# A relational graph convolution on one core: edge counts per group alone on TensorE, counts per relation from the slot table

## The chip, the cores and the metric

The kernel runs on one core of a Trainium2 chip. The core has five engines with a queue each, which run at the same time and wait for each other through semaphores: TensorE (PE in the profile; its weight loads are PEld), VectorE (DVE), ScalarE (ACT), GpSimd (POOL) and SyncE (SP, which here only starts transfers). Matrix products are written by TensorE into PSUM, which has eight banks, and are read from there by VectorE and ScalarE. The metric is the device time of one execution in microseconds; the time before is the median of three executions.

## The reference

For 1250 nodes with 1024 features and 20,000 edges of 8 relations, the kernel computes one graph layer with a gate and a residual. Cut to what matters:

```
h = relu(layernorm(x))
u = h @ root + bias
for r in range(8):
    mask = (edge_type == r)
    sums = segment_sum(h[src] * mask, dst)          # over the edges of relation r
    cnt  = segment_sum(mask, dst)                   # edges of relation r into each node
    u   += (sums / max(cnt, 1)) @ weight[r]
z = concat([u, h]) @ w_gate + b_gate
out = x + tanh(u) * z + h * (1 - z)
```

The edges are only known at run time, so the kernel sorts them itself: that is its index.

## The kernel before

**Products.** The kernel multiplies first and gathers then: for every relation it forms y = h @ weight[r] for all nodes (and h @ root, h @ w_gate), stores the rows of y in HBM, and each node then gathers the rows of its edges and adds them with the weight 1/cnt. There are eleven matrices of 1024 x 1024 (eight relations, root, two halves of the gate), numbered s. The ten blocks of 128 nodes go in five pairs, numbered i. One (s, i) is a `step`; its product is done with Strassen's seven half-size products, partly nested a second time (lines 210 to 360), in fp32. A step calls `between(j)` after each of its sub-products; there the generators that stand for all other work (the index, later the gathering) are moved on by one `yield`. What a generator issues between two yields thus lands in every engine's queue right behind that sub-product. The order of every queue is the program's own order; nothing reorders it.

**Two groups.** Relations 0 to 4 are group 0, relations 5 to 7 group 1 (`R0 = (0, 5, 8)`), so that gathering from group 0 can run while group 1 is multiplied. Each (group, node) is a key. Each key has a row of `SLOTS` = 28 places in a table in HBM; an edge's place is key x row width + the edge's rank among the edges of its key. The row of the table had 8 more words (`WIDE` = 36), into which the reciprocals of the relation counts were stored.

**The index.** `columns` prepares the edges as 157 columns of 128 edges: `key_col`, `row_col` (which row of y) and `tb_col` (relation x 10 + block of the target node). `slots` then goes over the columns in 40 rounds of `CG` = 4. For one group j of four columns it issues, over several rounds:

- `one_hots`: ScalarE makes `is_lo` (which of 128 low parts of the key), VectorE makes `is_at` (which of 20 high parts, line 1020, and which of 80 relation-blocks, line 1020 too).
- `count`: TensorE multiplies the one-hots, 4 matmuls of 100 columns (line 1031), into PSUM bank `ps_n`: the edges of each key and of each relation and node in each column. VectorE adds them to the running sum `seen` (line 1036), four additions, one after the other.
- `as_int`, `split`, `as_bf16`: the running sum before each column is cut into two bf16 parts, with casts on ScalarE (1051, 1053, 1066) and two masks on VectorE (1059).
- `place`: TensorE looks the sums up for each edge, 4 matmuls of 40 columns (line 1082), into PSUM bank `ps_q`. VectorE picks each edge's own value (1087, 1091), counts the equal keys ahead of it in its column (1096), and forms its place `at_i` (1099 to 1106). GpSimd scatters the four columns into the table (1110). `at_i` has two buffers.

In one round the order is: `as_bf16(j-3)`, `one_hots(j)`, the load of the keys, `as_int(j-2)`, a yield, `count(j-1)`, `split(j-2)`, `place(j-3)`, `to_los(j-2)`, a yield. So on TensorE four count matmuls and four look-up matmuls, of different groups of columns, stand one behind the other. The rounds run beside the steps of s = 0 to 3, from about 107 to 417 us.

**After it.** `order` ranks the nodes by their number of edges, stores the reciprocals of the relation counts into the table (line 1149, SP) and gathers each node's table row, in rank order, into `idx`. `weights(g)` turns `idx` into a weight for each slot on VectorE (`slot_weights`, lines 730 to 743). From s = 5 on, `edges` gathers rows of y (line 1294, GpSimd) and adds them (line 1299, VectorE) beside the products. `passes_needed` works out whether a node has more edges than slots; a runtime branch (line 1441: every engine loads the number, line 1443: and branches) skips the code for that case, which this data doesn't need. `got()` hands out one of five scratch tiles.

## Time and profile before

| | |
|---|---|
| median of 3 runs | 1348.01 us (1346.19 to 1349.48) |
| profiled execution, its own time | 1347.63 us |
| its span, first to last instruction | 1345.6 us |
| VectorE, ScalarE, GpSimd busy | 74%, 29%, 43% of the span |
| VectorE busy in the index rounds, 107 to 417 us | 236.0 of 310.0 us |
| ScalarE busy in the same stretch | 177.2 of 310.0 us |
| VectorE busy from 417 to 506 us, and from 506 to 625 us | 49.8 of 89.0 us, and 59.4 of 119.0 us |
| GpSimd's table scatters end; its next work starts | 419.8 us; 457.1 us |
| first gather of y rows | 635.1 us |
| granted TensorE clock, mean | 0.998 |

A line of a timeline has the start in us, the busy time in us, the engine, the source line, the operation, the tile written and the tiles read, sizes, the number of instructions merged, and in brackets how long the engine had been idle and what released it. A line of the groups has the same names, then busy time in us and the mean duration of one instruction in ns, and the idle time before them by releaser. A matmul's duration includes its way through the array: matmuls overlap, so what one costs TensorE is the distance to the start of the next.

### The profile page before, as it was taken

How to read it: one execution, taken by the hardware profiler on the slowest of the kernel's cores; microseconds unless marked ns; L12 is line 12 of the kernel's file. 1: busy time of each engine (PE TensorE's matmuls, PEld its weight loads, DVE VectorE, ACT ScalarE, POOL GpSimd, SP SyncE). 2: the span in 40 equal slices, each digit the busy share in tenths (PEclk: the TensorE clock that was granted, in tenths of full speed). 3: DMA queues.
4: the chain of work that ended last, by engine and by line, in shares of the span. 5: the costliest groups of instructions: out<-in, count | busy, mean ns of one | idle time of the engine just before them, and what ended most of it. 6: DMA issues, size and time to landing. Idle time of an engine off the chain costs nothing.

```text
span 1345.6 us, 13662 instructions
## 1 busy us (share of the span) xinstructions
PE 1332.0 (99%) x4098; PEld 712.2 (53%) x4098; DVE 995.7 (74%) x2049; ACT 384.0 (29%) x852; POOL 579.9 (43%) x511
## 2 busy tenths in 40 slices
PE   9999999999999999999999999999999999999997
PEld 5444455455445545655654565565556556554443
DVE  7855976876784937524887978887788799867875
ACT  3335656565641111111221211112122111221210
POOL 0001755655563346101444646336354655625631
PEclk9999999999999999999999999999999999999999
DMA  8744665844673162133739778867878967879961
GB/s 313 271 181 145 105 135 148 209 81 124 160 183 83 49 171 53 48 126 122 234 114 349 223 254 326 310 230 268 286 260 291 343 211 234 288 275 283 345 171 59
DMA packets 106910, 271.17 MB, mean 202 GB/s; under 512 B 22692, under 2 KB 24946, under 8 KB 106704
## 3 DMA queue, kind: packets, MB, share of 16 engines
q1 hardware_dynamic: 46640, 120.01, 29.2%
q0 software_dynamic: 44064, 118.28, 27.9%
q10 hardware_dynamic: 16128, 31.98, 7.2%
q8 instruction: 32, 0.52, 0.2%
q14 instruction: 46, 0.38, 0.1%
HBM read 212.71 MB, written 75.66 MB: 214 GB/s over the span
## 4 chain that ended last, share of the span: by engine, by line
PE 79%; issue 7%; DMA 7%; DVE 4%; POOL 3%; ACT 0%; POOLq 0%; DVEq 0%; ACTq 0%
PE ps_b L405 40%; PE ps L405 17%; PE ps L218 11%; DMA got<-y,idx 5%; PE ps_n L405 3%; PE ps_b L218 2%; PE ps_q L218 2%; PE ps_q L405 1%; DVE u L1299 1%; PE ps_n L218 1%; POOL got L1294 1%; DMA got<-hr_dram,node 1%; PE ps L370 1%; DMA hr_dram<-row 1%; POOL out_dram L720 1%
## 5 line engine op out<-in xcount | busy, mean ns | idle before, releaser
L405 PE MATMUL ps_b<-w,h_op 128*128 128x512 f32 x1560 | 701.9, 595 | 1.0 <-ACT row L484 0.8
L405 PEld LDWEIGHTS ps_b<-w,h_op 128*128 128x128 f32 x1560 | 291.6, 190 | 329.2 <-issue 318.7
L1294 POOL DMA_INDIRECT got<-y,idx x193 | 246.3, 1276 | 326.4 <-DVE u L1299 195.8
L1299 DVE SCALAR_TENSOR_TENSOR u<-got,w_of,u 128x1024 f32<-128x1024 f32 (+1 forms) x193 | 247.1, 1283 | 33.8 <-DMA got<-y,idx 31.1
L405 PE MATMUL ps<-w,h_op 128*128 128x512 f32 (+1 forms) x592 | 263.4, 588 | 1.0 <-ACT row L464 1.0
L1110 POOL DMA_INDIRECT table<-row_col,at_i x157 | 177.7, 1132 | 156.4 <-DVE at_i L1106 70.3
L405 PEld LDWEIGHTS ps<-w,h_op 128*128 128x128 f32 x592 | 111.3, 190 | 125.0 <-issue 120.8
L430 DVE TENSOR_TENSOR row<-row 128x512 f32<-128x512 f32 x53 | 36.7, 693 | 72.9 <-ACT row L429 72.7
L429 ACT COPY row<-ps_b 128x512 f32<-128x512 f32 x53 | 31.0, 585 | 197.4 <-PE ps_b L405 193.4
L514 ACT COPY row<-ps_b 128x512 f32<-128x512 f32 x49 | 28.6, 584 | 200.3 <-PE ps_b L405 171.5
L405 PE MATMUL ps_n<-w,h_op 128*128 128x512 f32 x176 | 80.1, 592 | 0.0
L218 PE MATMUL ps<-w,w 128*128 128x256 f32 x288 | 71.5, 381 | 0.3 <-DVE w L211 0.3
L484 ACT COPY row<-ps_b 128x512 f32<-128x512 f32 x54 | 31.6, 586 | 135.9 <-PE ps_b L405 131.1
L218 PE MATMUL ps<-w,h_op 128*128 128x256 f32 x264 | 68.3, 381 | 0.0
L218 PEld LDWEIGHTS ps<-w,w 128*128 128x128 f32 x288 | 54.2, 190 | 21.9 <-issue 14.6
L1036 DVE TENSOR_TENSOR seen<-seen,ps_n 128x100 f32<-128x100 f32 x157 | 40.3, 257 | 30.1 <-PE ps_n L1031 10.1
L218 PEld LDWEIGHTS ps<-w,h_op 128*128 128x128 f32 x264 | 49.6, 190 | 24.3 <-issue 18.7
L1096 DVE SCALAR_TENSOR_TENSOR junk<-k_bc,key_col,before 128x128 f32<-128x128 int32 x157 | 55.1, 351 | 4.2
L453 ACT COPY row<-ps_b 128x512 f32<-128x512 f32 x54 | 31.7, 587 | 90.9 <-PE ps_b L405 82.9
L405 PEld LDWEIGHTS ps_n<-w,h_op 128*128 128x128 f32 x176 | 33.4, 190 | 39.5 <-issue 38.7
L464 ACT COPY row<-ps 128x512 f32<-128x512 f32 x37 | 21.6, 585 | 105.2 <-PE ps L405 92.6
L173 DVE TENSOR_TENSOR w<-w,w 128x2048 f32<-128x2048 f32 (+1 forms) x12 | 25.4, 2115 | 35.1 <-PE ps L405 34.9
(244 smaller groups left out, 1530.6 us busy)
## 6 DMA issues: line engine op xcount, KB each, us to landing
y<-row SPq DMA_DIRECT2D x72, 512.0 KB
w<-in_L_gnn_weight_dram ACTq DMA_DIRECT2D x21, 1024.0 KB
w<-in_L_gnn_weight_dram SPq DMA_DIRECT2D x10, 1024.0 KB
k_bc<-keys_dram SPq DMA_DIRECT2D x39, 256.0 KB
l_bc<-los_dram SPq DMA_DIRECT2D x39, 256.0 KB
w<-in_L_gnn_w_gate_dram ACTq DMA_DIRECT2D x6, 1024.0 KB
h_dram<-h_op SPq DMA_DIRECT2D x9, 512.0 KB
u<-in_L_gnn_bias_dram SPq DMA_DIRECT2D x9, 512.0 KB
```

The costliest lines, as they stand in the source:

```text
L218: nc.tensor.matmul(p, a[:, k, :], b[:, k, :], start=(fresh and k == 0), stop=(k == 1), skip_group_check=True)
L405: nc.tensor.matmul(b[:, at], aop[:, i, k, :], w.of[i][:, k, at], start=(fresh and k == 0), stop=(k == KQ - 1), skip_group_check=True)
L429: nc.scalar.copy(d, b)
L430: nc.vector.tensor_add(c22, c22, d)
L453: nc.scalar.copy(c11, b)
L484: nc.scalar.copy(c12, b)
L514: nc.scalar.copy(c21, b)
L1036: nc.vector.tensor_add(seen[j][:, i, :], was, p[:, i, :])
L1096: nc.vector.scalar_tensor_tensor(junk, o["k_bc"][:, i, :], key_col[:, c:c + 1], before, op0=OP.is_equal, op1=OP.mult, accum_out=rank[:, c: ...
L1110: ins = nc.gpsimd.indirect_dma_start(out=table[:, :], out_offset=bass.IndirectOffsetOnAxis(ap=at_i[:n, i:i + 1], axis=0), in_=row_col[:n, ...
L1294: nc.gpsimd.indirect_dma_start(out=t[:n], out_offset=None, in_=y[g][:, :], in_offset=bass.IndirectOffsetOnAxis(ap=at[:n, d, k:k + 1], axis=0),
L1299: nc.vector.scalar_tensor_tensor(u[:n], t[:n], w, u[:n], op0=OP.mult, op1=OP.add)
```

## The change

The count matmul keeps the 20 columns of the keys only. The counts per relation are no longer made on TensorE; they come from the table rows in `idx`: since the table holds row numbers of y, which grow with the relation, the number of slots with a value of at least r x 1250 is counted on VectorE for each relation (`slot_counts`, one compare and one reduction each). Edges beyond the 28 slots are added by `counts_over`, behind a second runtime branch at the last step of s = 4. `tb_col`, the reciprocals in the table and their stores are gone; the table's row is 28 words. The running sum's two bf16 parts are now a rounded copy (ScalarE) and the rest (VectorE, `residue`). The last small operations of the rank are done for four rounds at once (`to_table`, `AT` = 4), and `at_i` is one tile for all columns. Counts and look-ups both write to parts of one PSUM bank, `q_bank` (the bank `ps_q`).

The rounds, as a diff:

```diff
+        q_bank = psum.tile([P, CG, P], F32, name="ps_q", bufs=1).rearrange("p c k -> p (c k)")
...
+            counted = q_bank[:, H:H + CG * NHI].rearrange("p (c b) -> p c b", b=NHI)
+            looked = q_bank[:, H + CG * NHI:H + 3 * CG * NHI].rearrange(
+                "p (c a b) -> p c a b", a=2, b=NHI)
...
@@ -1014,28 +1024,23 @@
                                          bias=less_lo[:, c0 + i:c0 + i + 1])
                 nc.scalar.activation(is_lo[:, :m, :], is_lo[:, :m, :], AF.Relu, scale=-1.0,
                                      bias=1.0)
-                is_at = ix.tile([P, CG, NHI + NTB], BF16, name="is_at", bufs=4)
-                for t, of, width in ((is_at[:, :, :NHI], hi_col, NHI),
-                                     (is_at[:, :, NHI:], tb_col, NTB)):
-                    nc.vector.tensor_tensor(t[:, :m, :],
-                                            of[:, c0:c1, None].to_broadcast([P, m, width]),
-                                            io[:, None, :width].to_broadcast([P, m, width]),
-                                            op=OP.is_equal)
+                is_at = ix.tile([P, CG, NHI], BF16, name="is_at", bufs=4)
+                nc.vector.tensor_tensor(is_at[:, :m, :],
+                                        hi_col[:, c0:c1, None].to_broadcast([P, m, NHI]),
+                                        io[:, None, :NHI].to_broadcast([P, m, NHI]),
+                                        op=OP.is_equal)
                 now[j] = dict(is_lo=is_lo, is_at=is_at)
 
             def count(j):
                 cs, o = chunks(j), now[j]
-                m = len(cs)
-                p = psum.tile([P, CG, P], F32, name="ps_n", bufs=1)[:, :, :NHI + NTB]
-                for i in range(m):
-                    nc.tensor.matmul(p[:, i, :], o["is_lo"][:, i, :], o["is_at"][:, i, :],
+                for i in range(len(cs)):
+                    nc.tensor.matmul(counted[:, i, :], o["is_lo"][:, i, :], o["is_at"][:, i, :],
                                      start=True, stop=True)
-                seen[j] = ix.tile([P, CG, NHI + NTB], F32, name="seen", bufs=3)
-                for i in range(m):
-                    was = seen[j][:, i - 1, :] if i else seen[j - 1][:, CG - 1, :]
-                    nc.vector.tensor_add(seen[j][:, i, :], was, p[:, i, :])
+                for i, c in enumerate(cs):
+                    nc.vector.tensor_add(seen[:, c % RING, :], seen[:, (c - 1) % RING, :],
+                                         counted[:, i, :])
                 if j == ng - 1:
-                    nc.vector.tensor_copy(runs, seen[j][:, m - 1, :])
+                    nc.vector.tensor_copy(runs, seen[:, cs[-1] % RING, :])
 
             def load_keys(j):
                 c0, m = j * CG, len(chunks(j))
@@ -1044,26 +1049,26 @@
                     nc.sync.dma_start(t[:, :m, :].rearrange("p c e -> p (c e)"),
                                       of[None, c0 * P:(c0 + m) * P].to_broadcast([P, m * P]))
 
-            def as_int(j):
+            def parts_seen(j):
 
                 m = len(chunks(j))
-                s_i = now[j]["s_i"] = ix.tile([P, CG, NHI], I32, name="s_i")
-                nc.scalar.copy(s_i[:, 0, :], seen[j - 1][:, CG - 1, :NHI])
-                if m > 1:
-                    nc.scalar.copy(s_i[:, 1:m, :], seen[j][:, :m - 1, :NHI])
-
-            def split(j):
-                m, o = len(chunks(j)), now[j]
-                s_2 = o["s_2"] = ix.tile([P, CG, 2, NHI], I32, name="s_2")
-                for a, mask in enumerate((-P, P - 1)):
-                    nc.vector.tensor_single_scalar(s_2[:, :m, a, :], o["s_i"][:, :m, :], mask,
-                                                   op=OP.bitwise_and)
+                k = (j * CG - 1) % RING
+                return [(0, k, 1), (1, 0, m - 1)] if k == RING - 1 else [(0, k, m)]
 
             def as_bf16(j):
 
-                m, o = len(chunks(j)), now[j]
-                s_b = o["s_b"] = ix.tile([P, CG, 2, NHI], BF16, name="s_b")
-                nc.scalar.copy(s_b[:, :m], o["s_2"][:, :m])
+                s_b = now[j]["s_b"] = ix.tile([P, CG, 2, NHI], BF16, name="s_b", bufs=3)
+                for to, k, n in parts_seen(j):
+                    if n:
+                        nc.scalar.copy(s_b[:, to:to + n, 0], seen[:, k:k + n])
+
+            def residue(j):
+
+                s_b = now[j]["s_b"]
+                for to, k, n in parts_seen(j):
+                    if n:
+                        nc.vector.tensor_sub(s_b[:, to:to + n, 1], seen[:, k:k + n],
+                                             s_b[:, to:to + n, 0])
 
             def to_los(j):
 
@@ -1076,48 +1081,49 @@
             def place(j):
                 cs, o = chunks(j), now.pop(j)
                 m, c0 = len(cs), cs[0]
-                c1 = c0 + m
-                p = psum.tile([P, CG, P], F32, name="ps_q", bufs=1).rearrange("p c k -> p (c k)")
                 for i in range(m):
-                    nc.tensor.matmul(p[:, i * 2 * NHI:(i + 1) * 2 * NHI], o["to_lo"][:, i, :],
+                    nc.tensor.matmul(looked[:, i].rearrange("p a b -> p (a b)"),
+                                     o["to_lo"][:, i, :],
                                      o["s_b"][:, i].rearrange("p a b -> p (a b)"),
                                      start=True, stop=True)
-                q = p[:, :CG * 2 * NHI].rearrange("p (c a b) -> p c a b", a=2, b=NHI)
                 own = ix.tile([P, CG, 2, NHI], F32, name="own", bufs=1)
                 nc.vector.tensor_tensor(
-                    own[:, :m], q[:, :m],
-                    o["is_at"][:, :m, None, :NHI].to_broadcast([P, m, 2, NHI]), op=OP.mult)
-                o2 = ix.tile([P, CG], F32, name="o2")
-                nc.vector.reduce_sum(o2[:, :m], own[:, :m].rearrange("p c a b -> p c (a b)"),
-                                     axis=AX.X)
+                    own[:, :m], looked[:, :m],
+                    o["is_at"][:, :m, None, :].to_broadcast([P, m, 2, NHI]), op=OP.mult)
+                nc.vector.reduce_sum(base[:, c0:c0 + m],
+                                     own[:, :m].rearrange("p c a b -> p c (a b)"), axis=AX.X)
 
                 for i, c in enumerate(cs):
                     junk = ix.tile([P, P], F32, name="junk", bufs=1)
                     nc.vector.scalar_tensor_tensor(junk, o["k_bc"][:, i, :], key_col[:, c:c + 1],
                                                    before, op0=OP.is_equal, op1=OP.mult,
                                                    accum_out=rank[:, c:c + 1])
-                nc.vector.tensor_add(rank[:, c0:c1], rank[:, c0:c1], o2[:, :m])
-                over = ix.tile([P, CG], F32, name="over")
-                nc.vector.tensor_single_scalar(over[:, :m], rank[:, c0:c1], float(SLOTS),
-                                               op=OP.is_ge)
-                at = ix.tile([P, CG], F32, name="at")
-                nc.vector.tensor_add(at[:, :m], first[:, c0:c1], rank[:, c0:c1])
-                at_i = ix.tile([P, CG], I32, name="at_i")
-                nc.vector.scalar_tensor_tensor(at_i[:, :m], over[:, :m], float(FAR), at[:, :m],
+                if j % AT == AT - 1 or j == ng - 1:
+                    to_table(j // AT * AT * CG, c0 + m)
+
+            def to_table(c0, c1):
+                at = slice(c0, c1)
+                m = c1 - c0
+                nc.vector.tensor_add(rank[:, at], rank[:, at], base[:, at])
+                over = ix.tile([P, AT * CG], F32, name="over", bufs=1)
+                nc.vector.tensor_single_scalar(over[:, :m], rank[:, at], float(SLOTS), op=OP.is_ge)
+                where = ix.tile([P, AT * CG], F32, name="where", bufs=1)
+                nc.vector.tensor_add(where[:, :m], first[:, at], rank[:, at])
+                nc.vector.scalar_tensor_tensor(at_i[:, at], over[:, :m], float(FAR), where[:, :m],
                                                op0=OP.mult, op1=OP.add)
-                for i, c in enumerate(cs):
+                for c in range(c0, c1):
                     n = nedges(c)
                     ins = nc.gpsimd.indirect_dma_start(
                         out=table[:, :],
-                        out_offset=bass.IndirectOffsetOnAxis(ap=at_i[:n, i:i + 1], axis=0),
+                        out_offset=bass.IndirectOffsetOnAxis(ap=at_i[:n, c:c + 1], axis=0),
                         in_=row_col[:n, c:c + 1], in_offset=None,
-                        bounds_check=G * KEYS * WIDE - 1, oob_is_err=False)
+                        bounds_check=G * KEYS * SLOTS - 1, oob_is_err=False)
                     tc.declare_no_dep(ins.ins, query=no_wait, group="scatter", reason="each edge has its own slot")
                     tc.add_to_no_dep_group("scatter", ins.ins)
 
             for j in range(ng + 3):
-                for f, of in ((as_bf16, j - 3), (one_hots, j), (load_keys, j - 1), (as_int, j - 2),
-                              (None, None), (count, j - 1), (split, j - 2), (place, j - 3),
+                for f, of in ((one_hots, j), (load_keys, j - 1), (as_bf16, j - 2),
+                              (None, None), (count, j - 1), (residue, j - 2), (place, j - 3),
                               (to_los, j - 2), (None, None)):
                     if f is None:
                         yield
```

The end of the chain, cut:

```diff
+    def slot_counts(g, at, t, cum, to):
+        n = R0[g + 1] - R0[g]
+        nc.vector.memset(cum[:, :, 0:1], float(at.shape[2]))
+        for r in range(1, n + 1):
+            nc.vector.tensor_single_scalar(t, at, float(r * N), op=OP.is_ge)
+            nc.vector.reduce_sum(cum[:, :, r:r + 1], t, axis=AX.X)
+            yield
+        nc.vector.tensor_sub(to[:, :, R0[g]:R0[g + 1]], cum[:, :, :n], cum[:, :, 1:n + 1])
...
-                for g in range(G):
-                    ins = nc.sync.dma_start(
-                        table[g * KEYS * WIDE:(g + 1) * KEYS * WIDE]
-                        .rearrange("(d p s) o -> p d (s o)", p=P, s=WIDE)[:, :, SLOTS:],
-                        rc.bitcast(I32))
...
         def beside_group():
+            for _ in range(4):
+                yield
+            passes_over()
+            yield
+            yield from rows_and_weights(1)
+            yield
+            yield
             for g in range(G):
-                if g:
-                    yield from rows_and_weights(g)
-                    yield
-                    yield
-                weights(g)
+                yield from counts(g)
+
+        def weights_of_groups():
+            as_reciprocals()
+            yield
+            for g in range(G):
+                yield from weights(g)
                 yield
             yield from passes_needed()
...
+        def counts_over():
+            over = nc.values_load(n_over[0:1, 0:1], min_val=0, max_val=E // MORE,
+                                  skip_runtime_bounds_check_because="no more passes than edges")
+            with tc.If(over > 0):
...
             s, i = next(steps)
+            if (s, i) == (R0[1] - 1, NP - 1):
+                for _ in ready:
+                    pass
+                counts_over()
+                ready = weights_of_groups()
```

`passes_over` and `passes_needed` each transpose one column of `most` on TensorE, where `passes_needed` transposed two. `slot_weights` now yields after each relation.

## The prediction

> **What bounds the kernel now.** I read the page first, then TensorE's timeline through the index rounds, then VectorE's timeline of the same rounds, then the groups of instructions by shape.
>
> ```profile
> span 1345.6 us, 13662 instructions
> PE 1332.0 (99%) x4098; PEld 712.2 (53%) x4098; DVE 995.7 (74%) x2049; ACT 384.0 (29%) x852; POOL 579.9 (43%) x511
> ```
>
> TensorE works without a break; only what lengthens or shortens its own stream, or makes it wait, moves the end. TensorE's timeline at two rounds of the index:
>
> ```profile
> 121.85 0.34 PE L1031 MATMUL ps_n<-is_at,is_lo 128*128 128x100 bf16 x4
> 122.03 0.26 PE L1082 MATMUL ps_q<-s_b,to_lo 128*128 128x40 bf16 x4
> 122.14 3.68 PE L405 MATMUL ps_b<-w,h_op 128*128 128x512 f32 x8
> ...
> 383.68 0.34 PE L1031 MATMUL ps_n<-is_at,is_lo 128*128 128x100 bf16 x4
> 383.87 0.26 PE L1082 MATMUL ps_q<-s_b,to_lo 128*128 128x40 bf16 x4
> 383.97 3.68 PE L405 MATMUL ps<-w,h_op 128*128 128x512 f32 x8
> ```
>
> Four count matmuls take 122.03 - 121.85 = 0.18 us (45 ns each), four look-up matmuls 0.105 us (26 ns each), and the look-ups follow the counts at once: they write another bank (ps_q) than the counts (ps_n). VectorE, the same two rounds:
>
> ```profile
> 122.05 2.29 DVE L173 TENSOR_TENSOR w<-w,w 128x2048 f32<-128x2048 f32 x1 [5.02 <-PE ps L405]
> 124.26 1.13 DVE L1036 TENSOR_TENSOR seen<-seen,ps_n 128x100 f32<-128x100 f32 x4
> ...
> 384.50 0.69 DVE L430 TENSOR_TENSOR row<-row 128x512 f32<-128x512 f32 x1 [2.19 <-ACT row L429]
> 385.11 2.29 DVE L177 TENSOR_TENSOR w<-w,w 128x2048 f32<-128x2048 f32 x1
> 387.31 1.13 DVE L1036 TENSOR_TENSOR seen<-seen,ps_n 128x100 f32<-128x100 f32 x4
> ```
>
> The four additions that read the counts run when VectorE gets to them: 2.3 and 3.5 us after the last count matmul started (121.99 and 383.82), behind evacuations and weight sums. Today nobody on TensorE waits for them. The groups by shape, for durations:
>
> ```profile
> L1036 DVE TENSOR_TENSOR seen<-seen,ps_n 128x100 f32<-128x100 f32 x157 | 40.3, 257 | 30.1 <-PE ps_n L1031 10.1 <-issue 6.2 <-remote 4.6
> L1020 DVE TENSOR_TENSOR is_at<-tb_col,io 128x320 bf16<-128x320 f32 x39 | 18.9, 486 | 0.0
> L1087 DVE TENSOR_TENSOR own<-ps_q,is_at 128x160 f32<-128x160 f32 x39 | 12.3, 316 | 0.2
> ```
>
> And the one long wait in these rounds, on TensorE and on VectorE:
>
> ```profile
> 354.93 0.26 PE L1082 MATMUL ps_q<-s_b,to_lo 128*128 128x40 bf16 x4 [1.36 <-ACT s_b L1066]
> ```
>
> ```profile
> 354.51 0.16 DVE L1106 SCALAR_TENSOR_TENSOR at_i<-over,at 128x4 int32<-128x4 f32 x1 [1.70 <-DMA table<-row_col,at_i]
> ```
>
> VectorE waited for scatters to release the at_i buffer, ScalarE's s_b came late behind it, and TensorE stood.
>
> **The change part by part.** *Counts 20 wide instead of 100.* The trace has no 20-wide matmul. The nearest row is the 40-wide look-up at 26 ns; on the straight line through 100 and 40 columns it would be about 20 ns, and no gain at all is the other bound. I take 26: 157 x 19 ns = **-3.0 us** (0 to -4).
>
> *The transposes of tb go*: from 46.83 to 47.26 us in TensorE's timeline, **-0.4 us**. *at_i becomes one tile for all rounds*: the wait at 354.93 had 1.53 us more than the usual step and a second one at 402.6 had 0.15: **-1.7 us** (0 to -1.7).
>
> *Counts and look-ups share one bank.* This is the term that matters. In the built program of the changed kernel the count and the look-up still stand one behind the other in TensorE's queue, but the first look-up matmul now carries a wait on VectorE's counter, and the value is the one that the last of the *same round's* four additions (line 1040 there) brings. This holds in 38 of the 40 look-up groups: the third count group to the last. So each round reads: four counts, VectorE finishes what stands ahead of the additions, four additions, four look-ups. All of TensorE's products queue behind the look-up, and ScalarE's and VectorE's evacuations wait for those. The price can be read from before, as the time from the start of the last count matmul to the end of the last addition, round by round. From the two timelines the first addition of these 38 rounds starts after (us)
>
> 2.27 0.73 3.63 1.01 2.41 2.36 0.24 2.24 1.29 0.92 0.25 1.29 0.24 0.25 0.24 1.29 0.24 2.32 0.72 0.25 0.25 3.18 1.07 1.28 0.46 0.67 0.25 0.24 0.67 0.99 0.24 1.78 0.67 0.25 0.24 3.50 0.24 1.23
>
> which is 41.4 us in sum; with the additions it is 1.38 to 4.75 us, 83.5 in sum.
>
> What shrinks of it: in eight rounds the 320-element one-hot of tb (0.48 us, gone) stood in that stretch, 3.6 us; the at_i wait in one round 1.2; small rank operations in one 0.3. Starts: 41.4 - 5.1 = **36.3 us**. The additions become 20 wide: 160 elements take 316 ns and 100 take 257, so 1 ns an element; 20 take 0.17 us, and the step from one to the next, (1.13 - 0.257)/3 = 0.29 us, becomes 0.21. Four take 3 x 0.21 + 0.17 = 0.80 us; 37 full rounds and one of one addition, **29.6 us**. The release costs about 0.05 us (the look-up at 354.93 began 0.05 after its ScalarE input was done), as much as the look-up today follows the last count, so it adds nothing. Together **+65.9 us**. Bounds: if the waiting TensorE lets VectorE work off all that is not itself released in that stretch, some 8.5 us of starts go (27.9) and the sum is 57; if nothing shrinks, it is 83.5.
>
> The Trainium skill has the rule behind that wait: "PSUM — Partial Sum Buffer", section "PSUM bank collisions raise a hardware error", says that PSUM is to be guarded by bank and partition group, not by address, since an engine reading one part of a bank while TensorE writes another part collides. The trace of before can't contradict it, as its reads and writes were in two banks. By addresses alone the new wait would cost 0; by the rule, which the built program follows, it costs the 65.9 us above.
>
> *VectorE and ScalarE work in these rounds.* Gone are the tb one-hot (18.9 us), some 80 ns of each of 157 additions, the two int32 masks (12.8 us), three of four small rank steps, and on ScalarE one of two casts (s_b from integers, 12.7 us). New is a subtraction of 80 elements a round, behind the additions (about 0.23 us by the 80-element one-hot, 9 us). From 107 to 417 us VectorE was busy 236.0 of 310.0 us and ScalarE 177.2. It is no bound, so by itself this is worth 0; its effect on the waits is counted above. Scatters in batches of 16 on GpSimd end later: 13 x 1.28 = 17 us after the last rank, about 435 instead of 419.8 us; GpSimd is idle till 457.10, so 0 (without that cover, the gather of idx at 488.30 would be late next). SP loses two rc stores (2.23 us of issue): 0.
>
> *New work later.* Eight compares and eight reductions over 280 elements (0.45 us each by the weights' rows) and two memsets: 7 to 8 us of VectorE between 506 and 625 us. In the slices from 538 to 639 us it is 50, 20 and 40% busy: 0; uncovered, 8 us spread over the evacuations. One transpose pair becomes two single transposes in different places: within 0.1 us. The gather of idx for the second group starts four calls later, about 12 us; it ended at 540.75 and its rows are wanted after 625: 0. *The second runtime branch*: the existing one read its register at 972.3 and branched at 972.9 on TensorE's queue, while matmuls started every 0.215 us at 973.32, 974.18 as without it: 0. SP's read took 1.3 us and GpSimd's join waits for open DMAs (none here): bound 0 to +2, taken 0.
>
> **Sum** on the profiled execution's 1347.63 us (span 1345.6, 2.0 around it): 1347.63 + 65.9 - 5.1 = **1408.4**. The median of the runs is 1348.01, 0.4 above that execution; I say 1408.
>
> **The rivals.** *(1) The waits keep their whole length*, because VectorE's backlog is set by products and not by its load: 14 rounds are at the floor already and the lumps of 2.29 us (L173, L177, L181) are released by TensorE or DMA. Against it: the tb one-hot visibly stood in the way. 1347.6 + 83.5 - 5.1 = 1426.
>
> *(2) The clock falls.* The granted clock is 1.00 in every stretch from 100 to 420 us, with no wait over 1.6 us; the first 24 matmuls of the kernel (L697, 128x128) took 0.21 us each against 0.11 for the same shape later, so a spell at half clock lost 24 x 0.10 = 2.5 us. Six rounds get a wait of 3 us or more. If each costs a spell: 1408 + 6 x 2.5 = 1423. Against it: nothing here shows that 3 to 4 us are enough in mid-kernel. The Trainium skill, "TensorE: Matmul & The Clock Gate", section "Why this matters for your kernels", warns of idle gaps over about 3 us; it would make all six count, the trace none.
>
> *(3) Not slower: the wait is there but already met when TensorE reaches it*, and the 5.1 us of gains remain: 1342.5. The point from which this decides: a mean wait under 5.1/38 = 0.13 us. For it: today's order has look-ups right behind counts at no cost. Against it: VectorE can't begin before the counts are done, its fastest start was 0.24 us, and four additions can't take under 0.6 us at 0.16 us (the smallest VectorE rows).
>
> *(4) VectorE catches up further than I count*: 1347.6 + 57 - 6 = 1399.
>
> **How the numbers follow.** Forecast (1400 to 1418) 0.64; waits at full length 0.12; clock falls in some or all 0.15; catch-up 0.06; not slower 0.03. The range 1397 to 1428 holds all but the last and the far tails. About 0.2% (2.7 us) can be told from no change: faster 0.02, same 0.01, slower 0.97.
>
> **What would show it.** After: look-up matmuls (L1085) in TensorE's waits with VectorE's additions (L1040) as releaser, 38 times, some 60 us in sum, 1.0 us in the shortest; index rounds end near 477 instead of 417 us; stages after it as long as before; PE share down to 94%; additions near 170 ns; counts about 26 ns apart; nothing at the new branch. Wrong would be: look-ups right behind the counts, or time lost after the index.

## The result, and the profile after

| | before | after |
|---|---|---|
| median | 1347.90 us (1346.19 to 1349.48) | 1477.12 us (1475.0 to 1482.08) |
| profiled execution, its span | 1347.63, 1345.6 us | 1478.27, 1476.5 us |
| last look-up matmul starts | 416.8 us | 544.1 us |

The ratio is 1.0964 (95% interval 1.0933 to 1.0996). The kernel is 129 us slower; 60 us were forecast, and the range ended at 1428 us. The page of the changed kernel, its busy times, two of its slices and three groups (names, total and mean, then the idle time before them):

```profile
span 1476.5 us, 13289 instructions
PE 1360.7 (92%) x4096; PEld 722.7 (49%) x4096; DVE 956.7 (65%) x1880; ACT 372.4 (25%) x786; POOL 559.7 (38%) x509
...
PE   9997887766678799999999999999999999999997
...
PEclk9999999888898899999999999999999999999999
...
L1116 POOL DMA_INDIRECT table<-row_col,at_i x157 | 160.6, 1023 | 316.6 <-DVE at_i L1112 230.3
L1085 PE MATMUL ps_q<-s_b,to_lo 128*128 128x40 bf16 x157 | 10.4, 183 | 100.9 <-DVE seen L1040 77.8
L1040 DVE TENSOR_TENSOR seen<-seen,ps_q 128x20 f32<-128x20 f32 x157 | 27.3, 174 | 105.4 <-PE ps_q L1037 64.0
```

The loss is where it was forecast, before the look-ups (L1085): TensorE's row is thin from slice 4 to 14. Behind the last look-up the kernel takes only 3.6 us more than before (932.4 against 928.8); a single wait of 3.6 us stands there, at 1207. But the loss is larger than forecast, and a second one lies beside it: the row of the clock has 8s in six of these slices. To size both I went through all matmuls from 9 us on and took the distance of each start from the one before, less what that distance is at full speed without a wait (429 ns for 512 columns, 215 for 256, 25 for the narrow ones).

- Before the look-ups the excess is **106.5 us** (before: 1.8). Eighteen of the 38 rounds are at the floor, that is at the shortest wait, 1.04 us; seven are between 4.3 and 10.1 us.
- In stretches at half clock, 15 of them besides one at the very end, the only one that before has after its first 7 us, the matmuls lose **28.8 us** more.
- The sum is 104.7 + 28.8 = 133.5; the measured difference is 130.6, so everything else gained 2.9.

TensorE's timeline at a floor round and at a long one:

```profile
216.19 0.25 PE L1037 MATMUL ps_q<-is_at,is_lo 128*128 128x20 bf16 x4
217.33 0.26 PE L1085 MATMUL ps_q<-s_b,to_lo 128*128 128x40 bf16 x4 [0.89 <-issue]
...
253.53 0.25 PE L1037 MATMUL ps_q<-is_at,is_lo 128*128 128x20 bf16 x4
263.71 0.29 PE L1085 MATMUL ps_q<-s_b,to_lo 128*128 128x40 bf16 x4 [9.93 <-DVE seen L1040]
```

The first is what the prediction described: VectorE free, additions, release. The second is not. VectorE and ScalarE at that round:

```profile
251.39 0.24 DVE L1028 TENSOR_TENSOR is_at<-hi_col,io 128x80 bf16<-128x80 f32 x1
262.86 0.80 DVE L1040 TENSOR_TENSOR seen<-seen,ps_q 128x20 f32<-128x20 f32 x4 [11.23 <-remote]
```

```profile
251.71 0.24 ACT L1063 CAST s_b<-seen 128x80 bf16<-128x80 f32 x1
262.80 0.58 ACT L452 COPY row<-ps_b 128x512 f32<-128x512 f32 x1 [10.84 <-remote]
```

VectorE has no backlog: it is idle for 11 us, and so is ScalarE, and both start at 262.8. Their instructions wait for TensorE alone, for products whose last matmuls started at 253.61 and 253.10. So TensorE's *completions reach the others 9 to 10 us late*; the trace's events of TensorE's semaphore stand at 262.77 and 262.83, none between 250 and 262. A profile models the end of a matmul, so these rows alone don't tell a product that is finished late from one that is only reported late; e1, below, says more on that. GpSimd in the meantime:

```profile
255.44 0.98 POOL L1116 DMA_INDIRECT table<-row_col,at_i  x1 [0.30 <-issue]
256.72 0.98 POOL L1116 DMA_INDIRECT table<-row_col,at_i  x1 [0.30 <-issue]
258.00 0.98 POOL L1116 DMA_INDIRECT table<-row_col,at_i  x1 [0.30 <-issue]
259.28 0.98 POOL L1116 DMA_INDIRECT table<-row_col,at_i  x1 [0.30 <-issue]
```

These are the last of a run of 16 scatters, one every 1.28 us, from 240.0 to 260.3. From here on I call an instruction of VectorE or ScalarE a *late start* if its engine had been idle for over 4 us and it began over 4 us after the start of the last matmul that it waited for. The trace of before has none (the longest is 2.24 us), that of the changed kernel nine, most near the end of a run of 16. The clock, by stretches (us, busy time and number of instructions of PE, PEld, DVE, ACT, POOL, then granted clock, DMA share, GB/s):

```profile
215.00:235.00 20.00, 17.77 (x64) 8.69 (x63) 6.69 (x34) 9.77 (x25) 4.71 (x5) 1.00 0.52 108
253.80:263.70 9.90, 0.00 (x0) 0.00 (x0) 0.74 (x5) 0.91 (x2) 4.94 (x6) 0.72 0.61 106
263.80:268.20 4.40, 4.40 (x9) 1.86 (x9) 3.25 (x15) 0.83 (x2) 0.00 (x0) 0.50 0.99 217
```

After the long wait the matmuls run at half clock: those of 512 columns in the last stretch start 0.85 us apart, where 0.43 is usual.

### The profile page after: what moved, and what is told of

Same layout as the page of the kernel before. It is cut to its first block, busy times and chain, and to the rows that moved or that the text cites. A ratio compares the mean times of both kernels' runs of the same rounds, so it can differ in the third digit from the quotient of the medians.

```text
span 1476.5 us, 13289 instructions
## 1 busy us (share of the span) xinstructions
PE 1360.7 (92%) x4096; PEld 722.7 (49%) x4096; DVE 956.7 (65%) x1880; ACT 372.4 (25%) x786; POOL 559.7 (38%) x509
## 3 DMA queue, kind: packets, MB, share of 16 engines
q0 software_dynamic: 44064, 118.20, 25.2%
## 4 chain that ended last, share of the span: by engine, by line
PE 76%; issue 7%; DVE 7%; another core or an unknown queue 4%; DMA 3%; POOL 2%; ACT 1%; POOLq 0%; DVEq 0%; ACTq 0%
PE ps_b L404 39%; PE ps L404 15%; PE ps L217 10%; PE ps_n L404 4%; PE ps_b L217 2%; PE ps_q L404 2%; PE ps_q L217 2%; DMA got<-y,idx 2%; DVE seen L1040 1%; PE ps_n L217 1%; PE ps L369 1%; POOL got L1300 1%; DVE u L1305 1%; PE ps_q L1085 1%
## 5 line engine op out<-in xcount | busy, mean ns | idle before, releaser
L404 PE MATMUL ps_b<-w,h_op 128*128 128x512 f32 x1560 | 713.6, 603 | 1.0 <-ACT row L483 0.8
L404 PEld LDWEIGHTS ps_b<-w,h_op 128*128 128x128 f32 x1560 | 296.1, 193 | 336.2 <-issue 325.8
L1116 POOL DMA_INDIRECT table<-row_col,at_i x157 | 160.6, 1023 | 316.6 <-DVE at_i L1112 230.3
L404 PE MATMUL ps<-w,h_op 128*128 128x512 f32 (+1 forms) x592 | 276.3, 612 | 3.4 <-ACT row L463 3.4
L404 PEld LDWEIGHTS ps<-w,h_op 128*128 128x128 f32 x592 | 116.7, 199 | 135.9 <-issue 129.1
L1085 PE MATMUL ps_q<-s_b,to_lo 128*128 128x40 bf16 x157 | 10.4, 183 | 100.9 <-DVE seen L1040 77.8
L1040 DVE TENSOR_TENSOR seen<-seen,ps_q 128x20 f32<-128x20 f32 x157 | 27.3, 174 | 105.4 <-PE ps_q L1037 64.0
L217 PEld LDWEIGHTS ps<-w,h_op 128*128 128x128 f32 x264 | 50.4, 193 | 24.5 <-issue 19.5
L1085 PEld LDWEIGHTS <-to_lo 128*128 128x128 bf16 x157 | 9.7, 97 | 104.7 <-issue 104.6
```

Source lines behind the costliest of these rows:

```text
L217: nc.tensor.matmul(p, a[:, k, :], b[:, k, :], start=(fresh and k == 0), stop=(k == 1), skip_group_check=True)
L404: nc.tensor.matmul(b[:, at], aop[:, i, k, :], w.of[i][:, k, at], start=(fresh and k == 0), stop=(k == KQ - 1), skip_group_check=True)
L1040: nc.vector.tensor_add(seen[:, c % RING, :], seen[:, (c - 1) % RING, :], counted[:, i, :])
L1085: nc.tensor.matmul(looked[:, i].rearrange("p a b -> p (a b)"), o["to_lo"][:, i, :], o["s_b"][:, i].rearrange("p a b -> p (a b)"), start=Tr ...
L1116: ins = nc.gpsimd.indirect_dma_start(out=table[:, :], out_offset=bass.IndirectOffsetOnAxis(ap=at_i[:n, c:c + 1], axis=0), in_=row_col[:n, ...
```

## Experiments: bank and batch

The kernels of a group ran on one chip, with the kernel before beside them. The first group undoes the two suspects apart and together.

**e1, two banks.**

```diff
+        n_bank = psum.tile([P, CG, P], F32, name="ps_n", bufs=1).rearrange("p c k -> p (c k)")
...
-            counted = q_bank[:, H:H + CG * NHI].rearrange("p (c b) -> p c b", b=NHI)
+            counted = n_bank[:, H:H + CG * NHI].rearrange("p (c b) -> p c b", b=NHI)
```

> As the changed kernel, but the counts write the bank ps_n again and only the look-ups write ps_q. Theory A (the shared bank makes TensorE wait before the look-ups, 106.5 us in the profile of the changed kernel, and these waits make the clock fall, 28.8 us): 1477 - 106.5 + 1.8 - 28.8 = 1343.5 us, between 1340 and 1347; the look-ups follow the counts at once, no spell of half clock between 100 and 540 us. Rival B (scattering in batches of 16 makes completions of TensorE reach the others up to 9 us late, and that costs time whatever the banks are): VectorE and ScalarE still start up to 9 us late near the end of a batch, TensorE then waits for a product's bank instead, and the time lies between 1360 and 1410 us.

**e2, one bank, four scatters a round** (`AT = 4` becomes `AT = 1`).

> As the changed kernel, one bank, but the ranks and scatters are done in every round (AT = 1, 4 scatters at a time instead of 16). Theory A2 (the seven waits of 4 to 10 us, 59 us in sum, come from the batches of 16, near whose end TensorE's completions reach VectorE and ScalarE late): no wait before the look-ups is over 5 us, their sum falls from 106.5 to about 55 us (50 to 65), the spells of half clock lose about 12 us instead of 28.8, time 1405 to 1420 us. Rival C (the long waits belong to the shared bank itself, whatever the scatters do): the long waits stay, sum near 105 us, time 1465 to 1480 us.

**e3, both edits.**

> Both undone: two banks, and four scatters in every round; what stays of the change is the narrow counts, the counts of relations from the slot table and the new parts of the sums. Theory A: equal to the kernel with two banks and batches of 16 within 3 us, 1340 to 1347 us. Rival B (batches cost time by themselves): this one is 15 to 60 us faster than that one. Rival D (the rest of the change has a price of its own, such as the second branch): more than 1350 us here too.

**e4, counts a sub-product ahead**, with one bank and batches of 16.

```diff
-                              (None, None), (count, j - 1), (residue, j - 2), (place, j - 3),
+                              (count, j - 1), (None, None), (residue, j - 2), (place, j - 3),
```

> As the changed kernel, one bank and batches of 16, but the counts are issued one sub-product of TensorE (3 to 4 us) earlier than the look-ups, so that the additions have that time. Theory A: the waits before the look-ups shrink to the part by which VectorE's additions are later than 3.7 us, about 5 us without the late completions, and up to some 35 us with them (seven times 5); the counts now wait for the multiplication that reads the looked-up sums, about 0 to 10 us; 1350 to 1400 us. Rival E (the shared bank costs its time wherever counts and look-ups stand): 1460 us or more.

| group 1, before 1349.12 us | median | ratio to before (95%) | runs of ten scatters or more | late starts | waits before look-ups, lost at half clock |
|---|---|---|---|---|---|
| changed kernel (measured apart) | 1477.12 | 1.0964 (1.0933 to 1.0996) | 8 | 9 | 106.5, 28.8 us |
| e1 two banks, batches of 16 | 1383.42 | 1.0250 (1.0210 to 1.0290) | 5 | 9 | 3.6, 10.6 |
| e2 one bank, four a round | 1414.87 | 1.0495 (1.0456 to 1.0534) | 0 | 0 | 60.4, 11.7 |
| e3 two banks, four a round | 1349.05 | 0.9989 (0.9968 to 1.0011) | 2 | 1 | 0.2, 1.5 |
| e4 one bank, batches, counts ahead | 1391.86 | 1.0322 (1.0283 to 1.0362) | 8 | 9 | 16.7, 11.0 |

A run is counted with no more than 1.5 us from one scatter to the next; the kernel before has none over 8. Two causes, then, and both theories of e1 were partly right. The **bank** costs 1414.87 - 1349.05 = 65.8 us with four scatters a round. The **batch** costs 1383.42 - 1349.05 = 34.4 us without the shared bank and 1477.12 - 1414.87 = 62.3 us with it. In e2 the long waits are gone; its waits by releaser (total, times, longest):

```profile
PE ps_q L1085 <- DVE seen L1040: 47.5, 32, 4.2
PE ps_q L1085 <- ACT to_lo L1078: 2.0, 1, 2.0
```

In e1 the late starts stay, and what TensorE waits for then is a bank that ScalarE should have emptied:

```profile
PE ps_b L404 <- ACT row L483: 9.4, 2, 8.6
PE ps_n L1038 <- DVE seen L1041: 5.4, 2, 4.4
```

The wait of 8.6 us, on TensorE and on ScalarE:

```profile
227.78 3.17 PE L404 MATMUL ps<-w,h_op 128*128 128x512 f32 x7
230.78 3.60 PE L404 MATMUL ps_b<-w,h_op 128*128 128x512 f32 x8
234.42 1.11 PE L217 MATMUL ps<-w,h_op 128*128 128x256 f32 x4
244.16 2.08 PE L404 MATMUL ps_b<-w,h_op 128*128 128x512 f32 x2 [8.63 <-ACT row L483]
```

```profile
240.97 0.58 ACT L463 COPY row<-ps 128x512 f32<-128x512 f32 x1 [10.95 <-remote]
```

ScalarE reads the product of the first line, whose last matmul started at 230.36, only from 240.97. Behind that matmul TensorE had started 20 more without a break by 235.5. So, as far as the starts can show it, the product was made in time and its report came late.

Without the shared bank TensorE has other products to go on with, so a late start of 10 us costs less; with it, TensorE stands from the first microsecond. e4 shows that the bank's price is one of place: with a sub-product between counts and look-ups most of it goes, and e4 lies 8 us over e1.

## Experiments: what in the batches

**e5, scatters issued four a round** while the ranks stay in batches of four rounds: `to_table` puts its columns in a list, and each round issues four.

> Two banks and ranks for four rounds at once as in the changed kernel, but the 16 scatters of a batch go out four in each of the next four rounds. Theory A2 (only the run of 16 scatters one behind the other does the harm): no completion of TensorE is over 6 us late, the time is that of the kernel with two banks and four ranks and scatters a round, 1344 to 1351 us. Rival F (the batched small rank steps, or that at_i is known late, are the harm): it stays near 1383 us.

**e6, idle scatters:** e3, and in every fourth round six scatters with every index at `FAR`.

> Two banks, ranks and scatters in every round, and in every fourth round six more scatters whose indices are all out of bounds, so that they write nothing: GpSimd then runs some 18 scatters one behind the other, while the writes that reach the table stay at four scatters a round. Theory G (GpSimd's long unbroken run of scatters makes the completions late, whatever they write): some completions 6 to 11 us late near the ends of the runs, 1370 to 1390 us. Rival H (the writes pile up, GpSimd's run is harmless): no completion over 6 us late but for the one or two seen without them, 1345 to 1353 us.

**e7, paced:** e1 with this ahead of each scatter.

```diff
+                    for _ in range(3):
+                        nc.gpsimd.memset(pause, 0.0)
```

> Two banks and batches of 16 as in the changed kernel, but GpSimd clears a small tile three times (about 0.6 us) ahead of every scatter, so that a batch goes out at one scatter in 1.9 us instead of 1.28 us; GpSimd is then at work nearly without a break. Theory G (the length of GpSimd's run): completions late as before or longer, 1380 us or more. Rival H (the rate at which the writes come): the late completions go or become short, 1345 to 1360 us.

**e8, two rounds at once:** e1 with `AT = 2`.

> Two banks, ranks and scatters for two rounds at once (runs of 8 scatters, 10 us). In the runs of 16 the late completions came in the last third of a run. Theories G and H alike: with 8 there are few or none, 1345 to 1357 us; if the harm goes with the number of scatters in a run in proportion, 1349 + 34 x 4 / 12 = 1360 us.

Group 2 gave, with 1345.41 us for the kernel before: e5 1342.51 us (ratio 0.9977, 0.9963 to 0.9990), e6 1347.13, e8 1341.85 (0.9979, 0.9962 to 0.9996). e7 took 1424.96, but 74.3 us of it is one wait: a scatter took 2.24 us with its pause, GpSimd ended them at 512.7, and the ranking behind them came late. No trace of the group had a start even 1.2 us late by the same measure. That looked like a success for spreading, but the trace of e5 spoke against it: GpSimd still worked off 11 to 16 scatters one behind the other at 1.28 us, since nothing in its own queue ties a scatter to a round. The edit had changed nothing there. So the kernels had to be compared side by side:

> The kernel with two banks and batches of 16, as before, now beside the one whose scatters are issued four a round. The trace of that one showed that GpSimd still worked off 11 to 16 of them one behind the other, with the same 1.28 us between them, and yet no late completion. Theory I (it is the chip or the moment: late completions come and go): this kernel has few late completions here too, about 1345 us. Theory J (it is the program, that is where the scatters stand in the order in which the instructions were written): late completions again, 1375 to 1390 us.

> Two banks, scatters issued four a round, beside the kernel with two banks whose scatters are issued 16 at once. Theory J: no late completion, 1340 to 1348 us again. Theory I: as the other one, within 5 us, wherever that lies.

> The changed kernel itself on the same chip as these two. Theory J: 1470 to 1485 us, seven waits of 4 to 10 us before the look-ups. Theory I: if the late completions are absent here, about the time with one bank and four scatters a round, 1408 to 1425 us.

Group 3 (before 1347.88 us): two banks 1391.00, spread 1388.85, changed kernel 1477.35 us. Twelve late starts in each of the first two: e5's edit is without effect, and the late starts are there in a whole group of runs or not at all. The same chip number stands in groups of both kinds, so the chip alone doesn't decide it; what does is open (the end of this section has a mark of it). Group 2 therefore says nothing of the batches, and its three questions were put again beside the changed kernel as a control. The pause is now two clears.

> The changed kernel as the control of this group. If the chip is one with late completions: 1470 to 1485 us. If it is one without: theory A2 says that only the 60 us of waits and some 12 us of clock stay, 1405 to 1420 us.

> Where the control is at 1470 us or more. Theory G (GpSimd's long unbroken run makes the completions late, whatever it writes): completions 6 to 11 us late, 1365 to 1390 us. Rival H (the writes that reach the table pile up): 1345 to 1355 us.

> One scatter in about 1.9 us (two small tiles cleared ahead of each) instead of 1.28 us, in an almost unbroken run; GpSimd ends its scatters some 30 us later, which costs one wait of 10 to 20 us at the end of the rounds that is not counted here. Where the control is at 1470 us or more. Theory G: many late completions, 1380 us or more besides that wait. Rival H (the rate at which writes come): none or short ones, 1345 to 1355 us besides that wait.

> Two banks, ranks and scatters for two rounds at once, runs of mostly 8 scatters. Where the control is at 1470 us or more: few or no late completions if they need a run of some 10 scatters, 1344 to 1357 us; in proportion to the run, 1349 + 34 x 4 / 12 = 1360 us or more.

| group 4, before 1346.86 us | median | usual step between scatters | runs of ten or more | late starts |
|---|---|---|---|---|
| e12 changed kernel, control | 1478.00 | 1.28 us | 9 | 7 |
| e13 idle scatters | 1414.14 | 1.28 us | 10 | 14 |
| e14 paced, two clears | 1384.53 | 1.98 us | 0, GpSimd hardly pauses | 0 |
| e15 two rounds at once | 1350.40 | 1.28 us | 0, mostly 8 | 1 |

e13 writes no more to the table than e3, which was as fast as the kernel before. Yet e13 takes 67 us more than before, and more than either theory expected. Its GpSimd, where `far_i` marks the scatters that write nothing, and VectorE:

```profile
416.81 0.98 POOL L1106 DMA_INDIRECT table<-row_col,far_i  x1 [0.30 <-issue]
418.10 0.98 POOL L1106 DMA_INDIRECT table<-row_col,far_i  x1 [0.30 <-issue]
419.39 0.98 POOL L1106 DMA_INDIRECT table<-row_col,far_i  x1 [0.30 <-issue]
420.68 0.98 POOL L1126 DMA_INDIRECT table<-row_col,at_i  x1 [0.30 <-issue]
```

```profile
413.57 0.23 DVE L1031 TENSOR_TENSOR is_at<-hi_col,io 128x80 bf16<-128x80 f32 x1
427.94 0.80 DVE L1043 TENSOR_TENSOR seen<-seen,ps_n 128x20 f32<-128x20 f32 x4 [14.14 <-remote]
```

The counts that this addition reads started at 416.04. So it isn't the writes that reach the table that pile up (rival H falls as it was put). The transfers as such are not ruled out: queue q0, which carries the scatters, moved 45984 packets in e13 and 44064 in e3, which is 32 for each of the 60 idle scatters, as many as a full one sends. e14's GpSimd works without a break, and yet VectorE follows the counts (262.18 in its trace) at once:

```profile
256.72 0.98 POOL L1120 DMA_INDIRECT table<-row_col,at_i  x1 [0.52 <-issue]
257.69 0.50 POOL L1118 MEMSET pause<- 128x128 bf16 x2
258.70 1.20 POOL L1120 DMA_INDIRECT table<-row_col,at_i  x1 [0.52 <-issue]
```

```profile
262.47 0.80 DVE L1042 TENSOR_TENSOR seen<-seen,ps_n 128x20 f32<-128x20 f32 x4 [0.48 <-PE ps_n L1039]
```

So it isn't the length of GpSimd's work either (theory G falls as it was put). No start in e14 was even 1.2 us late, and of its 1384.5 us 34.3 are the one wait for the ranking that was expected (10 to 20 us were), as GpSimd ended at 471. What both leave is the **pace over a length**: scatters at 1.28 us, some ten or more behind one another, whether they write or not. Whether GpSimd's issuing or the transfers do the harm isn't separated, since the pause slows both. The late starts go roughly with the number of runs of ten or more: none in e2 and one in e15, which have no such run (e15 is 3.5 us over before), one in e3 with two, nine in e1 with five, nine in the changed kernel and in e4 with eight, twelve in e9 with seven and in e10 with eight, fourteen in e13 with ten; but only seven in e12 with nine.

Last, a pause of one clear, alone and with four scatters a round:

> Two banks, batches of 16, one small tile cleared ahead of each scatter, so that one goes out in about 1.66 us. If the pace has to be under some 1.3 us to do harm: no completion over 3 us late, 1340 to 1347 us. If the harm falls off slowly with the pace: some completions 4 us late and more, 1350 to 1370 us.

> The same with ranks and scatters in every round. No completion over 3 us late and no wait before the look-ups; 1340 to 1346 us, 0.2 to 0.5% under the kernel before. If pacing does nothing more for four scatters at a time: 1349 us, the same as before.

> Two banks and batches of 16 at 1.28 us: the control. 1380 to 1395 us on a chip with late completions, about 1342 us on one without.

Group 5 (before 1345.66 us) had no late starts, as its control shows: e18 1343.36 us (0.9981, 0.9963 to 0.9998). So the middle pace (1.36 us as measured, not 1.66) stays untested where it matters. e16 took **1341.20 us (0.9963, 0.9949 to 0.9977)** and e17 1341.78 (0.9972, 0.9961 to 0.9982): both beat the kernel before by 4 us. In a group with late starts they weren't run, and neither was the changed kernel in a group without.

How much the kind of group decides is seen where the same kernel ran in both kinds: two banks took 1383.42 us (e1) and 1391.00 (e9) but 1343.36 (e18); with idle scatters 1414.14 (e13) but 1347.13 (e6); with two rounds at once 1350.40 (e15) but 1341.85 (e8). Even the kernel before took 1346.86 to 1349.12 us in groups 1, 3 and 4, and 1345.41 and 1345.66 in groups 2 and 5.

One mark tells the kinds apart in every trace: the number of updates of TensorE's semaphore that it holds. 684 matmuls make one each. The traces of groups 2 and 5 hold 683 to 686 updates. Those of the kernel before, of the changed kernel and of groups 1, 3 and 4 hold 631 to 653, e2 and e14 among them, which have no late start; of VectorE's updates 6 to 18% are missing there too. So late starts stand only in recordings that lose events. Whether the recording itself makes the completions late, or both have one cause, was not tested: every execution on record comes with a clock from the profiler, and none without it is there to compare.

## Why the prediction was wrong

*The shared bank, +65.9 us:* right in mechanism and place, and near in size. e2 against e3 gives 65.8. That it agrees so closely is partly luck: the waits of e2 are 60.4 us, and the half clock, which the forecast held as a rival, takes 11.7; e3 in turn has a wait of 3.2 us at 998 and 1.5 us of half clock behind it, which e2 hasn't. The floor of 1.04 us in 18 rounds of the changed kernel is the forecast's shortest wait (0.24 + 0.80), and an addition takes 174 ns (0.17 forecast). The 29.6 us of the forecast leave out the one addition of the last round, 0.17 us; nothing hangs on it.

*The step that failed: "Scatters in batches of 16 on GpSimd end later ... so 0".* I asked only when the scatters end and who needs the table. What they do to the others while they run wasn't asked. It is 62.3 us with the shared bank, which carries the time from e2's 1414.87, inside the range, to 1477.12. No row of before showed the mechanism clearly: it has runs of up to 8, and starts of VectorE and ScalarE up to 2.24 us late. Two hints were there. One is an idle time of VectorE that was ended by "remote", which the prediction passed over:

```profile
175.76 1.13 DVE L1036 TENSOR_TENSOR seen<-seen,ps_n 128x100 f32<-128x100 f32 x4 [4.59 <-remote]
```

The other is the wait at 354.93, which the prediction shows and reads wrongly. ScalarE there, in the trace of before:

```profile
354.07 0.58 ACT L484 COPY row<-ps_b 128x512 f32<-128x512 f32 x1 [3.44 <-PE ps_n L1031]
354.55 0.33 ACT L1066 CAST s_b<-s 128x160 bf16<-128x160 int32 x1
```

The cast of `s_b` began at 354.55, before `at_i` was done (354.67), so `at_i` didn't hold it up. It stood behind the copy of line 484, and that waited for TensorE: the last matmul of its product had started at 351.93, the semaphore's event came at 354.05, 2.1 us later, just behind a run of seven scatters (344.0 to 352.8). What the forecast counted as a wait for `at_i` was the late completion in small.

*Rival (2), the clock, at 0.15:* it happened. The rival counted six rounds of 3 us or more, 15 us. The changed kernel lost 28.8. All 14 of its waits of 1.97 us or more before the look-ups went with a stretch of half clock, and none of the 24 shorter ones (1.73 us and less) did. The length alone doesn't decide it: in e2 six of eight waits of 2.17 us or more did so, and two, of 3.15 and 2.18 us, passed without. The late starts added long waits, each with 7 or 10 us of half clock that began within it. Its mechanism should have been in the forecast: "nothing here shows that 3 to 4 us are enough" was no evidence against it.

*The gains, -5.1:* counts start 27 ns apart (253.53 to 253.61; 26 forecast). In the groups without late starts e5, e8 and e16 to e18 are 2.3 (e18) to 4.5 us (e16) under before; of e3's gain in group 1 nothing is left (it has the wait at 998 and one late start). Right in sign, a little too large.

*VectorE's load, the later counts and the second branch at 0:* right within that. e16 has them all and is faster than before.

The miss by terms, on the profiled executions (1478.3 against 1408.4): waits 104.7 instead of 64.2 (65.9 less the 1.7 of the at_i wait), +40.5; clock 28.8 instead of 0; the rest -2.9 instead of -3.4. Together 69.8.

## What to carry to other kernels

Before two uses share a PSUM bank, look for the place where the write of one stands close behind the read of the other: a sub-product between them took most of 94 us away, a second bank all. And a batch of indirect transfers isn't free just because its engine is idle: it cost 34 us here with two banks and 62 with one, though in other groups of runs nothing. Look at what the other engines' waits do while such a run goes out, and keep the run short or its pace slow. Price a wait on TensorE with the clock it costs, not by its length alone.

## What the runs showed of the hardware

- Some ten or more scatters, one in 1.28 us, hold up TensorE's completions for others by up to 12.7 us (e13) and 12.8 us (e9), in groups of runs whose traces lose events of semaphores, and not at all in the others. At 1.98 us they don't (e14). Which path is held up stays open; the trace shows only that events of TensorE's semaphore come late and together.
- The granted clock falls after waits shorter than I had believed. Of the waits before look-ups in three profiles of the changed kernel (e11 and e12 among them), all 30 of 3.15 us or more had a stretch at half clock begin 2.4 to 5.5 us after the last count had started; so had 11 of 12 between 1.97 and 2.18 us, and none of 1.83 us or less. Stretches last 3.41 us or multiples of it: mostly 3.41 behind a short wait, 6.83 to 13.65 behind a long one. The Trainium skill, "TensorE: Matmul & The Clock Gate", section "Why this matters for your kernels", warns of gaps over about 3 us; here waits of 2 us could be enough, while in e2 one of 3.15 us passed without.
- The rule on banks in the Trainium skill, "PSUM — Partial Sum Buffer", section "PSUM bank collisions raise a hardware error", is what the built program follows; e2 and e3 put a price on it here, 65.8 us for 38 waits.
